# A graph layer on one core: a reordered setup, a shorter end and three more picks

## The chip, the cores and the metric

The kernel runs on one core of a Trainium2 chip. The metric is the device time of one execution in microseconds (us); a comparison is of medians over several runs.

## What is computed

There are 6250 nodes with 64 features, 200000 edges sorted by destination, 32 attributes and 9 further numbers per edge. For every edge the kernel takes the source node's row, weighs it, projects it, and sums over the edges of a destination; a gate, a residual and a layer normalisation follow.

```python
w   = silu(edge_attr @ W1 + b1) @ W2 + b2                  # (E, 9)
msg = einsum('ef,em,fmg->eg', x[src], edge_sh * w, W_tp)   # (E, 64)
agg = segment_sum(msg, dst, N) / sqrt(16.0)                # AVG_DEG = 100000 / 6250
gamma, beta = split(silu(c_noise[:, None] @ Wn1 + bn1) @ Wn2 + bn2, 2)
out = layernorm(x + agg * (1 + gamma) + beta)
```

## The kernel before

The edges lie in 1563 tiles of 128 (one edge to a partition), and the tiles in 98 blocks of 16 (`KB`). A block's source rows come into `hs[g]`, 128 x 16 x 64, in three ways:

- Most tiles are fetched by GpSimd with an indirect DMA of 128 rows each (`gather`, L99). Gathers run ahead of use by up to `AHEAD` = 6 blocks, in seven buffers; a gather of block g needs the buffer of block g-7, which `windows` (L533) has to have read.
- In every fourth block from block 7 on, one tile's rows are fetched one by one from the SP queue (`load_rows`, L115), 32 rows in each of four blocks.
- The last `picked(g)` tiles of a block, up to `Q` = 4, are "picked" out of a copy of x that lies in SBUF (`xs_w`, split into a high and a low part): a source index is cut into a key (partition, and one of 7 groups) and a place `jl` (one of 7). `hots` (L485, VectorE) compares the key of each edge with partition numbers and gives seven one-hot matrices `hot_k`; `pick` (L500, TensorE) multiplies them with `xs` in 14 matmuls of 448 columns into `px`; VectorE masks with `jl` (L509) and reduces (L511) into `hs`. `px` has two buffers.

The rest of a block: `hidden` (L429) and `hidden_act` (L438) are the first layer of the edge network, `second` (L447, L450) the second, `weights` (L457 to L467) turns and multiplies it into `a`, with the one-hot place of the destination in a window of 7 nodes (`near`, L408, from `rel`). `windows` (L533, L543) multiplies each tile's rows with `a`; `project` (L573, L579) applies W_tp to a pair of blocks, `halves` and `marks` make `r` and the one-hot `hot`, `place` (L595) puts the sums of a pair in their node columns, transposed, adding what the pair before carried over (`carry`, `yt`), and `bring` (L612) turns them back to nodes on partitions, where `finish` does gate, residual and normalisation and stores.

The order of instructions on each engine is the order of the program text (`manual_schedule`). Iteration i of the block loop issues the gathers of block i+6, the keys and `hots` of block i+2, pick 0 of block i+1 with the node work `nodes(i)` between its matmuls, `hidden(i+2)`, `second(i+1)`, `windows(i)`, `project` for odd i, and the other picks of block i+1.

The key table: `keys_of` works the keys out on VectorE in ten operations. Those of blocks 0 and 1 are spread over partitions by a matmul with `ones` (`keys_first`); those of all other blocks are transposed in three parts (`keys_rest`), written to DRAM (`kd`), and read back for two blocks at a time, spread over partitions (`load_keys`); `keys` copies them into PSUM. `setup` does all of this before the loop begins, together with the split of x (`split`, L247, L248), the first three picks (those of block 0), the tables for the window start of each block (`nid`, from `first_f`, `sel`, `lo`), and `rel` of all blocks.

At the end, after the picks of block 97, the pair (95, 96) is projected and placed, `bring` finishes two node tiles, and then block 97 goes the same way alone for the last node tile.

Of the kernel before, what the change touches and what calls it, by code (L numbers as in the profile page):

```python
# [7 lines left out]
F32 = mybir.dt.float32  # L8
# [8 lines left out]
P = 128  # L17
# [6 lines left out]
W = 7  # L24
# [27 lines left out]
def picked(g):  # L52

    return Q - (g % 5 == 0)
# [13 lines left out]
def gnn_resnorm_kernel(ctx: ExitStack, tc: tile.TileContext, x, src, dst, dst_row, ea, sh, cn,  # L68
# [18 lines left out]
    with ExitStack() as fast:  # L87
# [58 lines left out]

        def setup(temp):
# [12 lines left out]
            row_i = xb.rearrange("p j f -> p (j f)")[:, 0:NBLK * KB].bitcast(I32)  # L160
            load(0, split=True)
            nc.sync.dma_start(dst_i[:, 0:2 * KB], dst[:, 0:2 * KB])
            nc.sync.dma_start(row_i[:, 0:2 * KB], rows(dst[0, 0:2 * KB], P))
# [5 lines left out]
            for c in range(KB // 4):  # L169
                q = c * D  # L170
                nc.sync.dma_start(b2c[q:q + 2 * M, :], bass.AP(tensor=b2.tensor, offset=b2.offset,
                                                               ap=[[0, 2], [1, M], [1, 1]]))
            first_i = temp.tile([NBLK, KB], I32)
            nc.sync.dma_start(first_i, dst[0].rearrange("(g k) -> g k", k=KB))
            cn_j = temp.tile([NJ, P], F32)
            nc.sync.dma_start(cn_j, cn)

# [4 lines left out]
            sel_i = temp.tile([KB, P], I32)  # L182
# [5 lines left out]
            for g in range(AHEAD):  # L188
                gather(g)

# [6 lines left out]
            nc.vector.tensor_copy(li, n_i[:, 0:J])  # L197
            ones = temp.tile([P, P], F32)
            nc.vector.memset(ones, 1.0)


            zt_r = ztw

            def keys_of(g0, g1):

                c0, c1 = g0 * Q, g1 * Q
                s_f, kp, kh, rest, t0, t1 = [zt_r[:, k * C + c0:k * C + c1] for k in range(6)]
                ti = [t.bitcast(I32) for t in (t0, t1)]
                g2 = min(g1, NBLK - 1)
                nc.vector.tensor_copy(s_f[:, 0:(g2 - g0) * Q].rearrange("p (g k) -> p g k", k=Q),  # L210
                                      src_i.rearrange("p (g k) -> p g k", k=KB)[:, g0:g2, KB - Q:])
                if g1 == NBLK:
                    nc.vector.tensor_copy(s_f[:, (g2 - g0) * Q:], src_i[:, NT - Q:NT])
                nc.vector.tensor_scalar(ti[0], s_f, 2675.0, None, op0=ALU.mult)
                nc.vector.tensor_scalar(ti[0], ti[0], 17, None, op0=ALU.logical_shift_right)
                nc.vector.tensor_copy(kp, ti[0])
                nc.vector.scalar_tensor_tensor(rest, kp, -float(J * J), s_f, op0=ALU.mult, op1=ALU.add)
                nc.vector.tensor_scalar(ti[1], rest, 37.0, None, op0=ALU.mult)
                nc.vector.tensor_scalar(ti[1], ti[1], 8, None, op0=ALU.logical_shift_right)
                nc.vector.tensor_scalar(kh, ti[1], float(P), None, op0=ALU.mult)  # L220
                nc.vector.tensor_add(s_f, kp, kh)
                nc.vector.scalar_tensor_tensor(jl[:, c0:c1], kh, -float(J) / P, rest, op0=ALU.mult, op1=ALU.add)
                return s_f

            def keys_first(g, kf, tag):

                pk_t[g] = psum.tile([P, Q, P], F32, tag=tag, name=f"pk{g}")
                for t in range(picked(g)):
                    c = (g + 1) * Q - picked(g) + t
                    d0 = NBLK * KB + c * P  # L230
                    dg = xb.rearrange("p j f -> p (j f)")[:, d0:d0 + P]
                    nc.vector.tensor_scalar(dg, ident, kf[:, c:c + 1], None, op0=ALU.mult)
                    nc.tensor.matmul(pk_t[g][:, t, :], ones, dg, start=True, stop=True)  # L233

            def keys_rest(kf):
                for c0 in range(LB * Q, C, P):
                    n = min(P, C - c0)
                    p_kt = psum.tile([P, P], F32, tag="r", name=f"p_kt{c0}")
                    nc.tensor.transpose(p_kt[0:n], kf[:, c0 - LB * Q:c0 - LB * Q + n], ident)
                    kt = zt_r[:, 6 * C + c0 // 2:6 * C + c0 // 2 + P // 2].bitcast(F16)  # L240
                    nc.scalar.copy(kt[0:n], p_kt[0:n])
                    nc.sync.dma_start(kd[c0:c0 + n, :], kt[0:n])


            def split(h):
                xh = gam[:, h * J:(h + 1) * J, :].rearrange("p l f -> p f l")
                nc.scalar.copy(xs[0][:, h], xh)  # L247
                nc.vector.tensor_sub(xs[1][:, h], xh, xs[0][:, h].bitcast(F32))  # L248

            kf = keys_of(0, LB)  # L250
            keys_first(0, kf, "r")
            hots(0, 0, 1)
            for h in range(J):
                split(h)
                if h == J // 2:
                    hots(0, 1, 2)
            one = temp.tile([1, 1], F32)
            nc.vector.memset(one, 0.0)
            nc.scalar.activation(one, one, AF.Silu)
            pick(0, 0)  # L260
            hots(0, 2, Q)
            hidden(0)
            keys_first(1, kf, "s")
            hots(1, 0, 1)
            nc.vector.tensor_copy(wi, n_i[:, 0:W])
            nc.vector.tensor_sub(rel[:, 0:2 * KB], dst_i[:, 0:2 * KB], row_i[:, 0:2 * KB])
            near(0)
            pick(0, 1)
            hots(1, 1, Q)
            second(0)  # L270
            pick(0, 2, [[lambda: None, lambda: None], weights(0)])
            hidden(1)

            nc.sync.dma_start(dst_i[:, 2 * KB:], dst[:, 2 * KB:])
            nc.sync.dma_start(row_i[:, 2 * KB:], rows(dst[0, 2 * KB:], P))
            load(LB)
            keys_rest(keys_of(LB, NBLK))
            load_keys(LB)
            for q in range(2):
                n = (M + 1 - q) // 2  # L280
                nc.sync.dma_start(wtc2[q * F:(q + 1) * F, 0:n, :], wtp[:, q:M:2, :])
            nc.vector.memset(wtc2[F:P, 4], 0.0)
            zero = temp.tile([P, 1], F32)
            nc.vector.memset(zero, 0.0)
            nc.scalar.copy(zt[F:P, :, 4].rearrange("p a k w -> p a (k w)"),
                           zero[F:P, :, None].to_broadcast([F, 4, KW]))
            nc.sync.dma_start(wn1c, wn1.rearrange("o h -> h o"))
            nc.sync.dma_start(bn1c, bn1.unsqueeze(1))
            nc.sync.dma_start(wn2a[0:H, :], wn2)
            nc.sync.dma_start(wn2a[H:H + 1, :], bn2.unsqueeze(0))  # L290
            row_f = temp.tile([P, len(SPG)], F32)
            nc.vector.tensor_scalar(row_f, src_i[:, SPG[0] * KB:NBLK * KB:SPS * KB], 4.0 * F, None, op0=ALU.mult)
            p_row = psum.tile([len(SPG), P], F32, tag="s", name="p_row")
            nc.tensor.transpose(p_row, row_f, ident)
            nc.vector.tensor_copy(row_a, p_row)
            first_t = temp.tile([NBLK, KB], F32)
            nc.scalar.copy(first_t, first_i)
            p_f = psum.tile([KB, NBLK], F32, tag="s", name="p_f")
            nc.tensor.matmul(p_f, first_t, ident[0:NBLK, 0:NBLK], start=True, stop=True)
            nc.scalar.copy(first_f, p_f)  # L300
            p_cn = psum.tile([P, NJ], F32, tag="r", name="p_cn")
            nc.tensor.matmul(p_cn, cn_j, ident[0:NJ, 0:NJ], start=True, stop=True)
            cn_s = temp.tile([P, NJ], F32)
            nc.scalar.copy(cn_s, p_cn)
            nc.sync.dma_start(cn_d, cn_s)
            gate_load(0)

            nc.vector.tensor_copy(lo, lo_i)
            sel_a = temp.tile([KB, P], F32)
            nc.vector.tensor_scalar(sel_a, sel_i, -0.5, None, op0=ALU.is_gt)  # L310
            sel = temp.tile([KB, P], F32)
            nc.vector.scalar_tensor_tensor(sel, sel_i, W - 0.5, sel_a, op0=ALU.is_lt, op1=ALU.mult)
# [6 lines left out]
            p_nid = psum.tile([P, NBLK], F32, tag="s", name="p_nid")  # L319
            nc.tensor.matmul(p_nid, sel, first_f, start=True, stop=True)  # L320
            nc.vector.scalar_tensor_tensor(nid, p_nid, pw, lo, op0=ALU.add, op1=ALU.subtract)
            nc.vector.tensor_add(ident2, ident[:, 0:F], ident[:, F:P])
            for k in range(2):
                nc.vector.memset(ht[k][H:H + 1], 1.0)
            nc.vector.memset(eps, EPS)

            nc.vector.tensor_sub(rel[:, 2 * KB:], dst_i[:, 2 * KB:], row_i[:, 2 * KB:])
            nc.vector.memset(rel[:, NT:], 0.0)
            if E % P:
                nc.vector.memset(rel[E % P:, NT - 1:NT], 0.0)  # L330
# [307 lines left out]
        with tc.manual_schedule(), tc.tile_pool(name="temp", bufs=1) as temp:  # L638
            setup(temp)

            for i in range(NBLK):
# [4 lines left out]
                if i % LB == 0 and i + LB < NBLK:  # L646
                    if i > 0:
                        load(i + LB)
# [261 lines left out]
```

## Time and profile before

| | |
|---|---|
| runs, median (3) | 1493.0 us (1492.52 to 1494.01) |
| profiled execution: own time, span | 2388.12 us, 2386.3 us |
| mean granted TensorE clock in it | 0.841 |
| busy: PE, PEld, DVE, ACT, POOL | 1675.3, 1367.1, 1206.6, 521.1, 1109.7 us |
| pick matmuls (L500), gathers (L99), row fetches (L115) | 5208, 1168, 2944 |
| DMA queue of SP (q1) | 52122 packets, 53.89 MB |

How to read it: PE is TensorE's matmuls, PEld its weight loads, DVE is VectorE, ACT ScalarE, POOL GpSimd, SP the queue of plain DMAs. A group's line gives line, engine, operation, out<-in and count, then busy time and mean ns of one, then idle time of the engine before it and what ended most of it. The profiled execution is 1.6 times as long as a run, so its spans aren't those of a run; its single durations are what is used.

### The profile page before, as it was taken

Reading aid. Unit: us, or ns where it says so; the run is one execution under the profiler, and the core shown is the slowest. Engines: PE = TensorE matmul, PEld = TensorE weight load, DVE = VectorE, ACT = ScalarE, POOL = GpSimd, SP = SyncE. Lnnn points to the kernel's source line nnn. Section 1 sums busy time; section 2 is a strip of 40 time slices with the busy share of each in tenths; the row PEclk is TensorE's granted clock in tenths of the full one; section 3 lists DMA queues with packets and bytes.
Section 4 is the critical chain, followed back from the end, with each engine's and each line's share of the span. In section 5 each row is a group of like instructions: output and inputs, shape, how many; then the busy total and the mean of one; then the engine's idle time right before and its main releaser. Section 6 shows DMA issues by size and latency. Waiting matters only on the chain. (4 is left out here: it accounts for less than half of the span.)

```text
span 2386.3 us, 34188 instructions
## 1 busy us (share of the span) xinstructions
PE 1675.3 (70%) x10858; PEld 1367.1 (57%) x10858; DVE 1206.6 (51%) x2157; ACT 521.1 (22%) x1326; POOL 1109.7 (47%) x1177
## 2 busy tenths in 40 slices
PE   3076777676776767677767677677777676877797
PEld 2065656564655655556656556565656564656586
DVE  3154545454545454545555545454545454545476
ACT  1021212121212121211222222121212121212133
POOL 7644444444444545444545454545444544444410
PEclk7598888888888988887888898788887888888898
DMA  3121111111111111111111111111111111111110
GB/s 114 34 62 40 47 34 41 36 46 37 38 35 42 41 39 38 44 37 38 35 36 44 38 37 45 35 36 35 47 34 37 36 45 35 37 35 46 33 38 5
DMA packets 90264, 96.13 MB, mean 40 GB/s; under 512 B 36744, under 2 KB 51290, under 8 KB 90074
## 3 DMA queue, kind: packets, MB, share of 16 engines
q1 hardware_dynamic: 52122, 53.89, 7.9%
q0 software_dynamic: 37376, 38.35, 7.1%
q8 instruction: 89, 1.46, 0.2%
q10 hardware_dynamic: 576, 1.61, 0.2%
q14 instruction: 101, 0.83, 0.1%
HBM read 92.01 MB, written 1.73 MB: 39 GB/s over the span
## 5 line engine op out<-in xcount | busy, mean ns | idle before, releaser
L99 POOL DMA_INDIRECT hs<-in_x_dram,src_i x1168 | 1108.4, 949 | 1167.6 <-PE pz L533 825.8
L500 PE MATMUL px<-xs_w,hot_k 128*128 128x448 f32 x5208 | 1304.3, 406 | 432.3 <-DVE xm L509 377.0
L500 PEld LDWEIGHTS px<-xs_w,hot_k 128*128 128x128 f32 x5208 | 1067.0, 213 | 567.4 <-DVE xm L509 409.5
L509 DVE SCALAR_TENSOR_TENSOR xm<-li,jl,px 128x448 f32<-128x448 f32 x372 | 251.8, 677 | 936.4 <-remote 698.0
L485 DVE TENSOR_TENSOR hot_k<-pk,nk 128x896 fp32r<-128x896 f32 x372 | 387.7, 1081 | 2.8 <-PE pk L233 2.8
L511 DVE TENSOR_REDUCE hs<-xm 128x64 f32<-128x448 f32 x372 | 230.6, 620 | 12.9
L438 ACT ACTIVATE st<-p,b1c 128x1024 f32<-128x1024 f32 x98 | 109.2, 1115 | 542.4 <-PE p L429 365.3
L543 ACT COPY ztw<-pz 64x140 f32<-64x140 f32 (+1 forms) x780 | 209.2, 268 | 21.7 <-PE pz L533 10.3
L447 PE MATMUL p<-st,w2p 128*32 128x256 f32 x784 | 71.8, 430 | 152.4 <-DVE xb L370 102.9
L601 ACT COPY carry<-ps 128x128 f32<-128x128 f32 x48 | 12.8, 266 | 649.4 <-PE ps L595 587.0
L533 PEld LDWEIGHTS pz<-a,hs 128*64 128x64 f32 x3116 | 116.5, 155 | 58.7 <-issue 55.1
L447 PEld LDWEIGHTS p<-st,w2p 128*32 128x32 f32 x784 | 17.6, 113 | 228.7 <-issue 127.1
L533 PE MATMUL pz<-a,hs 128*64 128x63 f32 x3116 | 131.7, 244 | 11.7 <-issue 11.5
L467 DVE TENSOR_TENSOR a<-oh,p 128x1008 f32<-128x1008 f32 x98 | 117.9, 1203 | 3.3
L429 PE MATMUL p<-ea,w1bd 64*128 64x512 f32 x392 | 111.5, 642 | 0.7 <-issue 0.7
L728 ACT ACTIVATE var<-var,eps 128x2 f32<-128x2 f32 (+1 forms) x25 | 7.4, 295 | 374.6 <-DVE var L725 374.6
L579 PE MATMUL pt<-ztw,wtc 128*64 128x112 f32 x960 | 71.9, 308 | 18.6 <-ACT st L438 18.6
L579 PEld LDWEIGHTS pt<-ztw,wtc 128*64 128x64 f32 x960 | 61.7, 170 | 20.6 <-ACT st L438 20.3
L554 DVE TENSOR_TENSOR r<-pt,r 112x128 fp32r<-112x128 f32 x48 | 13.9, 289 | 97.2 <-issue 86.2
L479 ACT CAST pk<-kr 128x512 f32<-128x512 f16 (+1 forms) x96 | 54.6, 569 | 16.5 <-DVE hot_k L485 11.1
L450 ACT ACTIVATE p2s<-p,b2c 128x256 f32<-128x256 f32 x98 | 45.9, 468 | 48.6 <-issue 30.5
L457 DVE STREAM_TRANSPOSE p<-p2s 128x256 f32<-128x256 f32 x98 | 44.1, 450 | 14.9 <-issue 14.4
(138 smaller groups left out, 552.7 us busy)
## 6 DMA issues: line engine op xcount, KB each, us to landing
hs<-in_x_dram SPq DMA_DIRECT2D x2944, 0.2 KB
ea<-in_ea_dram SPq DMA_DIRECT2D x48, 512.0 KB
hs<-in_x_dram,src_i POOLq DMA_INDIRECT x1168
kr<-kd SPq DMA_DIRECT2D x48, 256.0 KB
sh<-in_sh_dram SPq DMA_DIRECT2D x49, 144.0 KB
cb<-cn_d SPq DMA_DIRECT2D x12, 128.0 KB
out_dram<-o SPq DMA_DIRECT2D x24, 64.0 KB
dst_i<-in_dst_dram SPq DMA_DIRECT2D x1, 768.0 KB
```

The source lines that it names most:

```text
L99: hs_dma[g] = [nc.gpsimd.indirect_dma_start(out=hs[g][:, t - g * KB, :], out_offset=None, in_=x, in_offset=bass.IndirectOffsetOnAxis(ap=sr ...
L429: nc.tensor.matmul(p1[:, i, :].rearrange("p (c t e) -> p c t e", c=4, t=4), w1bd[i * 64:(i + 1) * 64, :], e[i * 64:(i + 1) * 64, :].rearra ...
L438: nc.scalar.activation(st[g], p1_t.pop(g), AF.Silu, bias=b1c)
L447: nc.tensor.matmul(p2[g][c * D:(c + 1) * D, 0, :].rearrange("p (i e) -> p i e", i=2), w2p, s[:, :, c * P:(c + 1) * P], start=True, stop=True)
L467: nc.vector.tensor_mul(a[g], oh_t.pop(g)[:, :, None, :].to_broadcast([P, KB, M, W]), sw.unsqueeze(3).to_broadcast([P, KB, M, W]))
L485: nc.vector.tensor_tensor(hot_k[g, t], pk_t[g][:, t, None, :].to_broadcast([P, J, P]), nk.unsqueeze(2).to_broadcast([P, J, P]), op=ALU.is_ ...
L500: nc.tensor.matmul(px.rearrange("p f l -> p (f l)"), hot_k[g, t][:, h, :], xs[i][:, h].rearrange("p f l -> p (f l)"), start=(h == 0 and i ...
L509: nc.vector.scalar_tensor_tensor(xm, li[:, None, :].to_broadcast([P, F, J]), jl[:, c:c + 1], px, op0=ALU.is_equal, op1=ALU.mult)
L511: nc.vector.tensor_reduce(hs[g][:, tiles(g) - q + t, :], xm, AX.X, ALU.add)
L533: mm = nc.tensor.matmul(pz[v][v * F:(v + 1) * F, k // 2].rearrange("p m w -> p (m w)"), hsg[:, k0 + k, :], ag[:, k0 + k].rearrange("p m w ...
L543: nc.scalar.copy(z[h * F:(h + 1) * F, 0:5 - h, k0 + v:k0 + n:2, :].rearrange("p m k w -> p k m w"), pz[v][v * F:(v + 1) * F, 0:(n + 1 - v) ...
L579: nc.tensor.matmul(pt[h * F:(h + 1) * F, 0, 0:KW], wtc2[:, c, :], z[h][:, c], start=(c == 0), stop=(c == 4))
```

## The change

It has five parts. `picked` leaves out one pick in every sixth block where it was every fifth. `keys_of` becomes a list of operations that work on a given buffer of six columns, `keys_rest` is replaced by `keys_turn`, one transpose of 128 keys; setup does only the keys of blocks 2 to 33, and those of 34 to 65 and 66 to 97 are worked out in iterations 2 and 4 of the loop, between picks, and transposed at the end of iterations 3 and 5. `rel` is worked out for blocks 0 and 1, then to block 9 in setup (`relative`), and for the others in iteration 6; its row numbers lie in `gam` instead of `xb`. `setup` takes in what was iteration 0 of the loop, so that the picks of blocks 0 and 1 stand among the setup's other work; `split` reads x in order and writes with a step, where it read with a step and wrote in order. At the end, block 97 is not placed and brought back: the sums of the pair (95, 96) and of block 97 are made by matmuls with `hot` as the stationary side, which gives nodes on partitions directly, and the last two node tiles are finished in one go.

```diff
-    return Q - (g % 5 == 0)
+    return Q - (g % 6 == 0)
...
+        def keys_turn(g0, kf, tag, kt):
+            c0 = g0 * Q
+            p_kt = psum.tile([P, P], F32, tag=tag, name=f"p_kt{g0}", bufs=1 + (tag == "pz"))
+            nc.tensor.transpose(p_kt, kf, ident)
+            nc.scalar.copy(kt, p_kt)
+            stores.append(lambda: nc.sync.dma_start(kd[c0:c0 + P, :], kt))
...
+        row_r = gam.rearrange("p j f -> p (j f)")[:, NBLK * KB:2 * NBLK * KB].bitcast(I32)
+        KC = P // Q
+        KN = 10 * KB
...
-            for g in range(AHEAD):
+            for g in range(AHEAD + 1):
                 gather(g)
...
             def split(h):
-                xh = gam[:, h * J:(h + 1) * J, :].rearrange("p l f -> p f l")
-                nc.scalar.copy(xs[0][:, h], xh)
-                nc.vector.tensor_sub(xs[1][:, h], xh, xs[0][:, h].bitcast(F32))
+                xh = gam[:, h * J:(h + 1) * J, :]
+                hi, lo_ = [xs[i][:, h].rearrange("p f l -> p l f") for i in range(2)]
+                nc.scalar.copy(hi, xh)
+                nc.vector.tensor_sub(lo_, xh, hi.bitcast(F32))
...
+            kb = [ztw[:, k * LB * Q:(k + 1) * LB * Q] for k in range(6)]
+            for f in keys_of(0, LB, kb):
+                f()
+            for f in keys_first(0, kb[0], "pz"):
+                f()
+            spread = keys_first(1, kb[0], "r")
...
+            hots(0, 0, 1)
+            for h in range(J):
+                split(h)
+            nc.scalar.activation(one, one, AF.Silu)
+            nc.sync.dma_start(dst_i[:, 2 * KB:], dst[:, 2 * KB:])
+            nc.sync.dma_start(row_r[:, 2 * KB:], rows(dst[0, 2 * KB:], P))
+            hots(0, 1, 2)
+            pick(0, 0, [spread[0:4], [lambda: hidden(0)]])
+            hots(0, 2, Q)
...
+            pick(0, 1)
+            second(0)
+            hots(1, 0, 1)
...
+            for f in keys_of(LB, LB + KC, kb):
+                f()
+            pick(0, 2)
+            hidden(1, act=False)
+            kt = temp.tile([P, P], F16)
+            keys_turn(LB, kb[0], "pz", kt)
+            hidden_act(1)
+            while stores:
+                stores.pop(0)()
+            load_keys(LB)
...
+            hots(1, 1, 2)
+            pick(1, 0)
+            nc.vector.tensor_copy(row_a, p_row)
+            nc.vector.tensor_sub(rel[:, 0:2 * KB], dst_i[:, 0:2 * KB], row_i)
+            near(0)
...
+            for f in weights(0):
+                f()
...
+            hots(1, 2, 3)
+            pick(1, 1)
...
+            windows(0)
+            second(1)
+            hots(1, 3, Q)
+            keys(2)
...
+            pick(1, 2)
+            hidden(2)
+            hots(2, 0, 1)
+            for f in weights(1):
+                f()
+            hots(2, 1, 2)
+            pick(1, 3)
+            relative(2 * KB, KN)
+            near(2)
+            hots(2, 2, Q)
...
+            more_of = {2: keys_of(LB + KC, LB + 2 * KC, kb), 4: keys_of(LB + 2 * KC, NBLK, kb),
+                       6: [lambda k=k: relative(KN + k, min(KN + k + 352, NBLK * KB))
+                           for k in range(0, NBLK * KB - KN, 352)]}
-            for i in range(NBLK):
+            for i in range(1, NBLK):
...
-                for t in range(2, Q):
-                    pick(i + 1, t)
+                beside = more_of.pop(i, [])
+                n = -(-len(beside) // (Q - 1))
+                for t in range(2, Q + 1):
+                    for f in beside[(t - 2) * n:(t - 1) * n]:
+                        f()
+                    if t < Q:
+                        pick(i + 1, t)
+                if i in (3, 5):
+                    keys_turn(LB + KC * (i - 1) // 2, kb[0], "s", kt)
...
-            pick(g, 2)
+            for f in bring(q - 2, q - 1, psum.tile([P, 1, F], F32, tag="r", name="py_l"), ends):
+                f()
+            windows(g - 1)
             sums(g)
-            windows(g - 1)
-            pick(g, 3)
-            marks(g // 2)
-            turn = project(g // 2)
+            pick(g, 2, [ends])
+            pick(g, 3, [project(q)])
...
+            py = psum.tile([P, FB, F], F32, tag="s", name="py_n")
+            nc.tensor.matmul(py[:, 0], carry.pop(q - 1), ident2, start=True, stop=False)
+            for b in range(2):
+                for k, h in enumerate(pair(q)):
+                    for s in range(2):
+                        nc.tensor.matmul(py[:, b], hot[h][:, b * P:(b + 1) * P], r[q][:, k, s],
+                                         start=(b == 1 and k == 0 and s == 0), stop=(b == 0 and k == 1 and s == 1))
+            windows(g, [0])
+            marks(NJ)
             windows(g, [ZT])
...
+            z = zs.pop(g).rearrange("p c k w -> p c (k w)")
+            pr = psum.tile([P, F], F32, tag="r", name="pr_n")
+            for c in range(5):
+                nc.tensor.matmul(pr[0:KW], z[:, c], wtc2[:, c, :], start=(c == 0), stop=(c == 4))
+            last = work.tile([KW, F], F32, tag="rt", name="last")
+            nc.vector.tensor_copy(last, pr[0:KW])
+            nc.tensor.matmul(py[:, 1], hot[g][:, 0:P].bitcast(F32), last, start=False, stop=True)
+            finish(q - 1, NJ, py)
```

Left out of the diff are the new places in the SP queue: the loads for blocks 2 and 3, W_tp and the gate's weights go out right after the first small loads, before the gathers are issued; the rest of `dst` and its row numbers follow the last split; the key part, `cn_d`, x for the residual (`xb`), `w2bd` and `b2r` follow within the picks of blocks 0 and 1. The tables `sel`, `pw` and `wi` move ahead of the first comparison, the rows of ones in `ht` are written by ScalarE instead of VectorE, and in `windows` of block 97 two of the copies of the second half go to VectorE.

## The prediction

> **What bounds the kernel now.** I read four views: the page, the waits, the timeline of the start and of the end, and a table of windows. First, the totals do not fit the runs: the profiled execution took 2388.1 us (span 2386.3, 1.8 around it), the runs 1493.0. The page and the waits say what the 895 us are.
>
> ```profile
> PE 1675.3 (70%) x10858; PEld 1367.1 (57%) x10858; DVE 1206.6 (51%) x2157; ACT 521.1 (22%) x1326; POOL 1109.7 (47%) x1177
> ...
> L99 POOL DMA_INDIRECT hs<-in_x_dram,src_i x1168 | 1108.4, 949 | 1167.6 <-PE pz L533 825.8
> L500 PE MATMUL px<-xs_w,hot_k 128*128 128x448 f32 x5208 | 1304.3, 406 | 432.3 <-DVE xm L509 377.0
> ```
> ```profile
> DVE xm L509 <- remote: 698.0, 119, 36.4
> ```
>
> PE is busy longer than a whole run lasts, and DVE waits 698 us for a releaser the trace cannot name. The timeline shows one such wait: PE has ended the pick's matmuls at 41.5, DVE reads them at 88.2.
>
> ```profile
> 36.33 5.16 PE L500 MATMUL px<-xs_w,hot_k 128*128 128x448 f32 x14
> ...
> 88.18 0.68 DVE L509 SCALAR_TENSOR_TENSOR xm<-li,jl,px 128x448 f32<-128x448 f32 x1 [36.45 <-remote]
> ```
>
> After such a wait PE is also slow: 14 matmuls in 5.16 us, against 3.05 at 20 us. So these waits belong to the profiled execution (1493 us has no room for them), and I take durations only where they are absent: the last 120 us, where PE has no gap.
>
> ```profile
> 2300.40:2314.50 14.10, 14.10 (x103) 11.90 (x102) 11.29 (x17) 3.87 (x12) 0.00 (x0) 1.00 0.25 67
> 2314.50:2330.00 15.50, 15.50 (x128) 13.13 (x127) 11.28 (x21) 4.82 (x15) 0.00 (x0) 1.00 0.00 1
> ```
> ```profile
> 2301.41 11.47 PE L500 MATMUL px<-xs_w,hot_k 128*128 128x448 f32 x56
> 2312.82 1.13 PE L429 MATMUL p<-ea,w1bd 64*128 64x512 f32 x4
> ```
>
> Columns of the first fence: stretch, its length, busy time of PE, PEld, DVE, ACT, POOL, clock. PE fills both blocks at clock 1.00. From the second: four picks (56 matmuls) run from 2301.41 to 2312.52 (0.3 us of gap before L429), so **a pick is 2.78 us of PE**. Between the pz of four blocks (2282.91 to 2341.69) lie 15 picks and 58.8 us: 14.70 a block, 14.84 at the kernel's 3.80 picks; one wait for an activation table load and st (1.6) in it, so 14.44 without. Blocks below 51 add the gate product (24.3 us in 49), 0.25 on the mean: 14.7 to 15.1.
>
> Two paths follow. **PE**: block loop from i=1 at 57.3 (worked out below), 95 blocks, then 33.3 from pick(97,0) at 2353 to the end, and 1.8: 1488 to 1526. **POOL**: gathers follow each other at 1.2534 us (mean of the 1075 unhindered intervals); 3.97 + 1168 x 1.2534 = 1468, 2 to land, then 14.7 from the last pz[0] to the end and 1.8: 1486.5. The median 1493 lies in the first and 6.5 above the second. So PE sets the end, POOL is close behind: its 14.9 a block gives it the rows of block i at about 19 + 14.9 i, PE asks at 48 + 14.75 i.
>
> **What the Trainium skill says.** "TensorE: Matmul & The Clock Gate", section "Wait — 56ns, not 53.3ns?": warm matmuls start N/2.4 GHz plus 2.5 ns apart, 189 ns for 448 columns, and cold ones at half the clock, 373. The trace: 198 in the last stage, 369 after the long wait. "DMA: Bandwidth & Descriptors", section "Anatomy of one DMA": some 2 us of a transfer are fixed, mostly the receipt of the write. No transfer's landing in this setup is measured in what I read; I use 2 us for the key table's way out to DRAM. "SBUF — State Buffer", section "Door 1: The DMA port swizzle": an access that crosses to a new 16-byte line pays. `split` reads at 256-byte steps now (0.93 us of DVE for 448 values, xm takes 0.68); afterwards it writes and re-reads at 28-byte steps, which cross too. No run shows that price.
>
> **Part 1: three more picks.** picked(g) sums to 372 now and 375 then (20 blocks short of one before, 17 after). PE: 3 x 2.78 = **+8.3**. DVE: 3 x (1.08 + 0.68 + 0.62) = 7.1, beside PE (DVE is busy 11.3 of 14.1 us in a block without finish). POOL: 3 gathers less, -3.8, off PE's path.
>
> **Part 2: the setup.** I lay out both orders with trace durations, without the long waits.
> Before: pick(0,0) ends on PE at 16.3. DVE then has xm and reduce of three picks (3.9), five hot_k (5.2), diagonals 0.9, near and small 0.7, weights(0) 2.2: 12.9, with 1.6 of waits for picks, 30.8. Key table of 384 columns, ten operations: 4.9, 35.7. Three transposes and ACT copies one behind the other on one PSUM tag (about 1 us each), kd written (2 us), read back: kr at about 44. Meanwhile DVE: row_a, nid behind p_f and p_nid, ht memsets 1.03, rel 1.75: 45.0. Then i=0: near 0.4, hot_k of block 2 4.2, xm(1,0) 1.3, weights(1) 2.2; PE ends pick(1,3) at **57.3**. Loop i=1 with project(0): 16.4, i=2: 14.9, so i=3 starts at 88.6.
> After: key diagonals of block 1, sel and pw lie in DVE idle time ahead of hot_k(0,0) (ends 9.0 for 8.8); seven splits in a row to 15.1; hot_k(0,1) 16.2. Then DVE is nearly solid: three xm 3.9, hot_k 2.1, keys of 128 columns 2.6, by 25.9; one hot_k, xm(1,0), row_a, rel of 32 columns, near, weights(0) by 33.1; two hot_k, xm(1,1), nid, by 37.1; xm(1,2), weights(1), two hot_k, xm(1,3) by 47.4; rel of 128 columns, near(2), hot_k(2,2..3), ident2 by 50.4. PE, ahead, ends pick(1,3) at **44.5**. The key table leaves at 25.4 and is needed at 37.1: its 4 to 5 us are covered by 11.7. PSUM tag "pz" holds pk0, p_kt, p_row, p_f, p_cn, p_nid in turn; windows(0) waits some 1.5 us for nid behind it, counted. The ht memsets go to ACT as two copies (0.6 each, by the 0.56 of zt's 448) ahead of st(2), while PE is in pick(1,2): hidden.
> Given back: DVE is 6 us behind PE, and pick(2,3) waits for xm(2,1). i=1 takes 18.2, i=2 15.1 (2.6 of DVE keys beside picks, DVE still 1.8 behind), so i=3 starts at 77.8: **10.8 earlier**. The keys at i=4 (2.6) and rel at i=6 (four of about 0.5) lie in DVE's 1.4 a block of room and the px buffers; if that cover is gone, up to 3. The two late transposes are 0.5 each on PE: **-9.8** in sum. Range -6 (splits slower by 0.3 each on DVE, kr at once before, the late keys uncovered) to -13 (splits at xm's 0.68, kr later before).
> SP: load(2), wtc and wn go out ahead of rest of dst and row; the write of a key third waits at the top of i=4 and i=6 for its copy, and behind it load(i+2) and 32 row fetches (10.8 us a block, L115) wait. Loads are for two blocks on, fetches for three to six: hidden, 1 us at most. The dst rest waits for the last split (gam is reused), 35 us ahead of use. POOL: the seventh group's gathers come from setup, same order, nothing.
>
> **Part 3: the end.** After pick(97,3) (PE 2366.5) the profile runs
>
> ```profile
> 2369.82 0.52 PE ps_l L595 x2
> ...
> 2371.01 0.66 PE py_l L612 x4
> ...
> 2373.49 2.14 PE pr L573 x10
> ...
> 2376.24 0.60 PE ps_n L595
> ...
> 2377.20 0.70 PE py_n L612 x2
> ```
> to 2386.3: 19.8 us, each step waiting for the one ahead (the chain of waits). After: xm and reduce 1.4, beside them carry, eight matmuls and windows(97,[0]), about 2.0; windows [8] 0.3; copies 1.1; pr 2.14; copy 0.25; last matmul 0.7; finish of two tiles 3.0 (as 2371.7 to 2374.7); store 5.9 as now (2380.4 to 2386.3): 15.5. Saved 4.3. But project(48) 1.2, its turn 0.3 and bring 0.35 move ahead of pick(97,3): +1.85. **-2.4**, bounds -1 to -3.5 (the eight products have no row; ps L595 takes 0.28 for 256 columns, I take 0.1 each).
>
> **Sum.** +8.3 - 9.8 - 2.4 = -3.9. Median 1493.0, so **1489**. Taken on the profiled 2388.1 the same edits would be 2384, but its remote waits (698 us) can move by more.
>
> **Rivals.**
> 1. PE as above: 1489, its own range 1484.5 (-13, -3.5) to 1494.5 (-6, -1, picks 8.6). For it: PE without a gap. Chance 0.5.
> 2. POOL already sets the end (gathers a little slower in a run than in the profile): then only its 3 x 1.25 and 0.5 of the tail count, 1488.7. Against: 6.5 us of room. Chance 0.17.
> 3. Start held up more than I laid out, as in the profile, where PE idles 42.6 to 93.9: the new order takes that away, up to where POOL binds: 3.97 + 1165 x 1.2534 + 2 + 14.2 + 1.8 = 1482. Against: the old kernel would then end beyond 1493. Chance 0.13.
> 4. Slower: DVE's debt is not paid. Each pick of i=1 to 6 waits in px (two buffers) for an xm behind hot_k, weights and keys; 5.2 us of keys and 1.9 of rel go on PE's path with setup's 6. s falls to 4, the end to -1.5: 8.3 - 5.5 = +2.8, 1496. It decides from s + e below 8.3 less 3.0. For it: DVE's 13.4 of 14.8 a block with finish and gates. Against: 1.4 a block repays. Chance 0.2.
> That the picks do not move is excluded: the sum over blocks is arithmetic.
>
> **Numbers.** About 0.2% (3 us) is what a measurement of this kernel tells from no change. Case 1 gives faster 0.32, same 0.17, slower 0.01; case 2 0.14 and 0.03; case 3 faster; case 4 same 0.04, slower 0.16: together 0.59, 0.24, 0.17. Range 1482 to 1497.
>
> **What would show it.** 5250 px matmuls and 1165 gathers; first pz L533 earlier against the number of picks ahead of it; PE without gaps in the last 100 us at 14.7 a block; from the last px to the end 15 to 16 us, with no ps or yt step. Wrong if DVE xm holds px in the first blocks beyond i=3, if splits take over 1.2 us, or if POOL no longer waits for pz near the end.

## The result, and the profile after

The changed kernel takes 1489.2 us (median of 20 runs, 1487.8 to 1494.1), the kernel before beside it 1493.3 (20 runs): ratio 0.9975, 95% interval 0.9969 to 0.9981, so 4 us less, against 3.9 predicted. In the first two sets of runs below every kernel, the one before included, took about 2400 us, in all others about 1490, on the same chip too, so each ratio is taken to the kernel before in the same set. The profiled execution took 1488.34 us with a span of 1486.5, that is 1.8 around it, at a mean granted clock of 0.994: unlike that of before, it is an execution like the runs, and its totals can be read.

On the page of the kernel after, first busy times, then the two groups that answer to those of before (busy, mean ns, idle before and releaser):

```profile
PE 1443.6 (97%) x10905; PEld 1211.5 (82%) x10905; DVE 1210.6 (81%) x2188; ACT 515.7 (35%) x1324; POOL 1108.5 (75%) x1174
...
L99 POOL DMA_INDIRECT hs<-in_x_dram,src_i x1165 | 1107.2, 950 | 357.1 <-issue 321.1
L536 PE MATMUL px<-xs_w,hot_k 128*128 128x448 f32 x5250 | 1125.2, 368 | 1.5 <-DVE hot_k L521 1.4
```

PE is busy for 97% of the span and the picks wait for next to nothing. But L99 tells of a second full queue: its 357 us of idle time are "issue", 0.3 us between one gather and the next, and no longer a wait for `pz`. GpSimd issues without a pause from 4.0 us to its last gather at 1465.2. Two queues are full at once here, and most of what the experiments showed follows from that.

In the waits of the kernel after (us in total, times, longest), the `remote` wait of 698 us is gone, and these are the two PE waits that come up again below:

```profile
PE pr L610 <- issue: 5.8, 1, 5.8
...
PE p L465 <- DMA ea<-in_ea_dram: 2.3, 2, 1.4
```

The timeline of PE in the kernel after, at the end (start, us, what, and the wait ahead of it):

```profile
1469.24 1.86 PE L536 MATMUL px<-xs_w,hot_k 128*128 128x448 f32 x8
...
1471.08 1.06 PE L743 MATMUL py_n<-r,c 112*128 112x64 f32 x8
...
1474.37 2.13 PE L751 MATMUL pr_n<-wtc,ztw 128*112 128x64 f32 x10 [1.40 <-ACT ztw L580]
1476.82 0.69 PE L754 MATMUL py_n<-last,c 112*128 112x64 f32 x2 [0.32 <-DVE last L753]
```

The `ps` and `yt` steps of before are gone; `py_n` is made by matmuls with `hot` (here `c`) directly. From the last pick (1471.1) to the end of the span (1486.5) pass 15.4 us, predicted 15.5.

### The profile page after: what moved, and what is told of

It reads as the page before. It is cut to its first block, busy times and chain, and to the rows that moved or that the text cites. A ratio compares the mean times of both kernels' runs of the same rounds, so it can differ in the third digit from the quotient of the medians.

```text
span 1486.5 us, 34308 instructions
## 1 busy us (share of the span) xinstructions
PE 1443.6 (97%) x10905; PEld 1211.5 (82%) x10905; DVE 1210.6 (81%) x2188; ACT 515.7 (35%) x1324; POOL 1108.5 (75%) x1174
## 3 DMA queue, kind: packets, MB, share of 16 engines
q1 hardware_dynamic: 52122, 53.89, 12.5%
## 4 chain that ended last, share of the span: by engine, by line
PE 79%; POOL 5%; DVE 5%; issue 4%; DMA 3%; ACT 3%; SPq 2%; ACTq 0%; DVEq 0%; POOLq 0%
PE px L536 60%; PE pz L569 6%; POOL hs L99 5%; PE p L465 5%; PE pt L616 3%; PE p L483 3%; DMA hs<-in_x_dram,src_i 2%; SPq L115 1%; ACT st L474 1%; DVE xm L545 1%; ACT L474 1%; PE ps L632 1%; DVE hs L547 1%; PE ps L661 1%; DVE hot_k L521 0%
## 5 line engine op out<-in xcount | busy, mean ns | idle before, releaser
L99 POOL DMA_INDIRECT hs<-in_x_dram,src_i x1165 | 1107.2, 950 | 357.1 <-issue 321.1
L536 PE MATMUL px<-xs_w,hot_k 128*128 128x448 f32 x5250 | 1125.2, 368 | 1.5 <-DVE hot_k L521 1.4
L536 PEld LDWEIGHTS px<-xs_w,hot_k 128*128 128x128 f32 x5250 | 961.2, 189 | 79.9 <-DVE xm L545 2.3
L569 PEld LDWEIGHTS pz<-a,hs 128*64 128x64 f32 x3116 | 99.6, 138 | 44.2 <-issue 39.3
L569 PE MATMUL pz<-a,hs 128*64 128x63 f32 x3116 | 112.8, 225 | 4.4 <-DMA hs<-in_x_dram,src_i 1.6
L483 PE MATMUL p<-st,w2p 128*32 128x256 f32 x784 | 62.6, 391 | 7.6 <-DVE xb L406 7.6
L616 PE MATMUL pt<-ztw,wtc 128*64 128x112 f32 x960 | 55.3, 261 | 3.1 <-ACT st L474 2.5
L465 PEld LDWEIGHTS p<-ea,w1bd 64*128 64x128 f32 x392 | 29.6, 185 | 31.5 <-issue 24.4
L497 DVE TENSOR_TENSOR p<-p,sh 128x72 f32<-128x72 f32 x196 | 47.3, 241 | 6.7
L616 PEld LDWEIGHTS pt<-ztw,wtc 128*64 128x64 f32 x960 | 46.8, 137 | 5.0 <-ACT st L474 3.9
```

The lines of the kernel that those rows point to most:

```text
L99: hs_dma[g] = [nc.gpsimd.indirect_dma_start(out=hs[g][:, t - g * KB, :], out_offset=None, in_=x, in_offset=bass.IndirectOffsetOnAxis(ap=sr ...
L465: nc.tensor.matmul(p1[:, i, :].rearrange("p (c t e) -> p c t e", c=4, t=4), w1bd[i * 64:(i + 1) * 64, :], e[i * 64:(i + 1) * 64, :].rearra ...
L483: nc.tensor.matmul(p2[g][c * D:(c + 1) * D, 0, :].rearrange("p (i e) -> p i e", i=2), w2p, s[:, :, c * P:(c + 1) * P], start=True, stop=True)
L536: nc.tensor.matmul(px.rearrange("p f l -> p (f l)"), hot_k[g, t][:, h, :], xs[i][:, h].rearrange("p f l -> p (f l)"), start=(h == 0 and i ...
L569: mm = nc.tensor.matmul(pz[v][v * F:(v + 1) * F, k // 2].rearrange("p m w -> p (m w)"), hsg[:, k0 + k, :], ag[:, k0 + k].rearrange("p m w ...
L616: nc.tensor.matmul(pt[h * F:(h + 1) * F, 0, 0:KW], wtc2[:, c, :], z[h][:, c], start=(c == 0), stop=(c == 4))
```

## The experiments

The sum of the prediction is tested by the last six experiments alone, at about 1490 us.

### The kernel before, profiled again

Edit: none.

> The kernel before, unchanged, to see one more profiled execution of it. My theory (the 895 us of the first profile are waits of that one execution): a span of about 1491 us, TensorE without long gaps, loop iteration 1 (first matmul of pick(2,0)) at 57 us and iteration 3 at 88.6; the last gather issued at about 1468 us and pz[0] of block 97 some 6 us after its rows have landed. Rival (the waits belong to the kernel): again above 2000 us, with VectorE waiting 36 us in the setup.

Measured: 2417.4 us, clock 0.831, the kernel before beside it 2423.0 in the median. Its waits (total, times, longest):

```profile
DVE xm L509 <- remote: 654.5, 112, 35.8
```

The wait came again, and the runs without a profile were as long. So it doesn't belong to the profiled execution alone, as the prediction had said, but to the whole set of runs. What holds PE's completions back there stays open: no run tells it apart.

### Parts of the change, where every kernel takes about 2400 us

The new numbers of picks in the kernel before, the old ones in the kernel after, and in the kernel after `pr` of a single block in another PSUM tag:

```diff
-    return Q - (g % 5 == 0)          # before, 375 picks (the kernel after with 372: the other way round)
+    return Q - (g % 6 == 0)
...
-                pr = psum.tile([P, 1, F], F32, tag="r", name=f"pr{q}")      # after, pr in p1
+                pr = psum.tile([P, 2, 4 * P], F32, tag="p1", name=f"pr{q}")[:, 0, 0:F].unsqueeze(1)
```

> The kernel before with the new pick count alone (375 for 372). TensorE sets the end (my theory): three picks more on its path, +8.3 us, about 1501.6. GpSimd sets the end (rival 2 of the prediction): three gathers less, -3.8 us, about 1489.5.

> The changed kernel with the old pick count (372). TensorE sets the end with GpSimd about 4 us behind (my theory after the changed kernel's profile: last gather at 1465.2, pz[0] of block 97 at 1472.1): TensorE would be 8.3 us earlier, GpSimd 3.8 later, so GpSimd takes over and the time stays within 1 us of 1489. TensorE alone: 1481. GpSimd sets the end already: +3.8, 1493.

> The changed kernel with the single-block product of project(0) in PSUM tag p1 in place of r. In the changed kernel's profile it starts at 53.95, 5.8 us after the pz of block 1, when hot_k of block 3 has been read out of the key tile that holds tag r. If that is the wait: it starts at about 49.6, TensorE is 4.3 us earlier from there, and since GpSimd leaves about 4 us at the end the time falls by 3 to 4 us, to about 1485.5. If GpSimd sets the end: no change, 1489. If the wait is for something else (weights, table): the product still starts at 54.

> The kernel before with the new pick count alone (375 for 372), again, on another occasion than e2. TensorE sets the end (my theory): three picks more on its path, +8.3 us on before. GpSimd sets the end (rival 2 of the prediction): three gathers less, -3.8 us. Its trace also shows the old setup and the old end: by my layout pick(2,0) starts on TensorE at 57 us, and 19.8 us lie between the last px and the end.

> The changed kernel with the product of project(0) in PSUM tag p1 in place of r, again, on another occasion than e4. If hot_k of block 3, reading the key tile in tag r, is what holds it for 5.8 us: it starts at about 49.6 in place of 53.95, TensorE is 4.3 us earlier from there, and as GpSimd leaves about 4 us at the end, the ratio to before falls from 0.9975 to about 0.995 (1485.5 us). If GpSimd sets the end already: 0.9975 as the changed kernel. If the wait is for something else, the product still starts at 54.

| | this, us | before, us | ratio, 95% interval |
|---|---|---|---|
| before, 375 picks | 2402.3 | 2423.0 | 0.9924 [0.9895, 0.9953] |
| after, 372 picks | 2424.4 | 2423.0 | 1.0032 [1.0009, 1.0054] |
| after, `pr` in p1 | 2409.8 | 2423.0 | 0.9938 [0.9914, 0.9961] |
| before, 375 picks, again | 2414.7 | 2420.5 | 0.9970 [0.9944, 0.9996] |
| after, `pr` in p1, again | 2412.3 | 2420.5 | 0.9972 [0.9942, 1.0002] |

Three more picks make the kernel before faster here, twice, where PE's sum says 8.3 us slower. Both forecasts of +8.3 missed; they were worked out for about 1490 us. Where DVE waits some 650 us in all for PE's completions, the end isn't set by PE's sum of durations, and these runs say nothing on that sum. The same edits follow at 1490 us.

### Picks alone, in both kernels

> The kernel before with the new pick count alone (375 for 372). TensorE sets the end (my theory): three picks more on its path, +8.3 us, ratio 1.0055. GpSimd sets the end (rival 2 of the prediction): three gathers less, -3.8 us, ratio 0.9975. Its trace also shows the old setup and the old end without long waits: by my layout pick(2,0) starts on TensorE at 57 us, pick(4,0) at 88.6, and 19.8 us lie between the last px and the end.

> The changed kernel with the old pick count (372), on a third occasion. In an execution near 1490 us: TensorE would be 8.3 us earlier and GpSimd 3.8 later, so GpSimd takes over and the ratio to before stays within 0.001 of 0.9975; if TensorE alone sets the end, 0.992; if GpSimd does already, 1.000. In an execution near 2400 us, as on the two occasions before: no more than 0.5% of difference, as e3.

The kernel before with 375 picks: 1501.7 us against 1493.0, ratio 1.0060 [1.0042, 1.0077], **+8.7** where 3 x 2.78 = 8.3 was worked out. PE sets the end of the kernel before, and a pick costs what its row says.

The kernel after with 372 picks: 1491.6 against 1493.7, ratio 0.9986 [0.9979, 0.9993]. PE has 8.3 us less to do than in the kernel after, and it gets **1.6 slower** (0.9986 against 0.9975; the two intervals just overlap). Within 0.001 of 0.9975 was expected, and both the 0.992 of PE alone and the 1.000 of GpSimd that sets the end already are excluded. In its profile PE waits 9.2 us in all ahead of `pz` after 1000 us, in the kernel after nothing. Here GpSimd, with 3 gathers more, has taken over. So the three picks aren't just a cost that the setup pays for: without them GpSimd caps what setup and end bring.

### How far behind PE is GpSimd?

Twelve more gathers, one in every second block from 30 to 52, into a tile that nothing reads:

```diff
+            if g in range(30, 54, 2):
+                nc.gpsimd.indirect_dma_start(
+                    out=more_rows[:, g // 2 % 4, :], out_offset=None, in_=x,
+                    in_offset=bass.IndirectOffsetOnAxis(ap=src_i[:, g * KB + 1:g * KB + 2], axis=0))
```

> The kernel before with 12 more gathers (blocks 30 to 52, every second; the rows go to a tile that nothing reads): 15.0 us more on GpSimd's queue, nothing on another engine. TensorE sets the end of the kernel before with GpSimd 6.5 us behind (my theory): +8.5 us, ratio 1.0057. GpSimd sets it (rival 2): +15, ratio 1.010. GpSimd has far more room than I worked out: 1.000.

> The changed kernel with the same 12 more gathers, 15.0 us on GpSimd's queue. TensorE sets the end with GpSimd 4 us behind: +11 on 1489.2, ratio to before 1.0049. GpSimd sets it: +15, 1.0075. TensorE alone with much room: 0.9975.

In the kernel before: 1507.6 against 1493.0, ratio 1.0094 [1.0077, 1.0112]. Of 12 x 1.25 = 15.0 us of gathers **14.6** come out. In the kernel after: 1502.4, ratio 1.0063 [1.0045, 1.0080], **13.2** more than its 1489.2. Both were expected to lose less. The first is the number forecast for rival 2 (GpSimd sets the end already), though three more picks have just shown PE to set it; the second interval takes in both of its forecasts. GpSimd has little room in either kernel, and a part of the loss is of another kind (below).

Where it binds can be read. I took for each block the start of its last gather on GpSimd and the first `pz` on PE. In the kernel before with 12 more gathers the waits ahead of `pz` from 1000 us on that the trace puts down to gathered rows lie at blocks 66, 70, 76, 80 and 90, and none after. The distance is least at or just behind the blocks divisible by 5 (in the kernel after: by 6): these have three picks, so a gather more, and PE comes a pick early and GpSimd a gather late. Block 97, where the prediction had closed GpSimd's path, has 7 gathers. The last gather of block 90 and its first `pz`, in the timelines of GpSimd and PE of that kernel, then the same of the kernel after with 372 picks, and of the kernel after; last, the same `pz` of the kernel before with 375 picks:

```profile
1384.01 0.94 POOL L99 DMA_INDIRECT hs<-in_x_dram,src_i  x1 [0.30 <-issue]
...
1387.36 1.98 PE L538 MATMUL pz<-a,hs 128*64 128x63 f32 x32 [2.71 <-DMA hs<-in_x_dram,src_i]
```
```profile
1373.21 0.94 POOL L99 DMA_INDIRECT hs<-in_x_dram,src_i  x1 [0.30 <-issue]
...
1376.77 1.15 PE L569 MATMUL pz<-a,hs 128*64 128x63 f32 x32 [2.90 <-issue]
```
```profile
1367.69 0.94 POOL L99 DMA_INDIRECT hs<-in_x_dram,src_i  x1 [0.30 <-issue]
...
1372.59 1.15 PE L569 MATMUL pz<-a,hs 128*64 128x63 f32 x32
```
```profile
1382.56 1.15 PE L533 MATMUL pz<-a,hs 128*64 128x63 f32 x32
```

From the gather's end (1384.95, 1374.15, 1368.63) to `pz` pass 2.4 us in the first, with a wait of 2.71; 2.6 in the second, with a wait of 2.90 that has no named releaser but lies at the same place; 4.0 in the third, with none. The shortest such distance in these traces is 1.7 us, and the longest at which `pz` was still waiting for rows is 2.9 (block 66 of the kernel after with 12 more gathers), so rows can be used 1.7 to 2.9 us after their gather's end. In this profile the kernel after has 1.1 to 2.3 us of room at block 90, and its loss of 13.2 of 15.0 (10.4 to 15.7 by its interval) fits.

For the kernel before it can be worked out. With the 15.0 taken off, its last gather of block 90 starts at 1369.0, and its rows are there at 1371.6 to 1372.8. From `pz` at 1382.56 to the end of the span at 1499.2 pass 116.6 us in the kernel before with 375 picks, which waits for no rows there (the picks from there on are as many); so PE, ending at 1493.0 less 1.8, was at block 90 at 1374.6. Room: **2 to 3 us, and not 6.5**.

A wait here can cost more than its length. The granted clock in four stretches around block 90 of the kernel before with 12 more gathers (stretch, length, busy time of PE, PEld, DVE, ACT, POOL, clock, DMA share, GB/s):

```profile
1382.00:1387.30 5.30, 2.65 (x18) 1.08 (x16) 5.27 (x7) 1.48 (x2) 4.08 (x5) 0.96 0.34 75
1387.30:1391.00 3.70, 3.64 (x37) 3.40 (x38) 1.82 (x4) 2.38 (x9) 2.78 (x4) 0.50 0.16 33
1391.00:1395.00 4.00, 4.00 (x15) 3.62 (x14) 0.57 (x1) 1.52 (x2) 3.03 (x4) 0.66 0.14 26
1395.00:1400.00 5.00, 5.00 (x26) 4.53 (x25) 2.03 (x4) 0.00 (x0) 3.78 (x4) 1.00 0.15 27
```

After 2.7 us of waiting PE runs at half its clock; `pz` and the 44 pick matmuls behind it take 13.2 us to their end at 1400.6, against 10.2 at full clock (1.08 and 9.08 in the kernel before with 375 picks). So 3 us follow the wait, and they aren't made good. The waits ahead of `pz` after 1000 us add up to 12.5, with these 3 that is 15.5; the profiled execution took 1509.3, which is 16.3 more than 1493.0, the median 14.6. Not every wait does this: in the traces with more gathers the clock stayed at 1.00 behind waits of 2.11, 2.16 and 2.26 us, and fell to 0.62 behind one of 2.15.

### The DVE debt

> The changed kernel with the product of project(0) in PSUM tag p1 in place of r. If hot_k of block 3, reading the key tile in tag r, is what holds it for 5.8 us: it starts at about 49.6 in place of 53.95, TensorE is 4.3 us earlier from there, and as GpSimd leaves about 4 us at the end, the ratio to before falls from 0.9975 to about 0.995 (1485.5 us). If GpSimd sets the end already: 0.9975, as the changed kernel. If the wait is for something else, the product still starts at 54.

Measured 1487.5 us against 1493.0, ratio 0.9960 [0.9945, 0.9974], faster than the kernel before. It is 1.7 us under the kernel after, which the overlapping intervals don't tell apart, where 3.7 was expected. PE in the kernel after, around the first `project`, with DVE's comparison that it waits for; then the same place with `pr` in p1:

```profile
47.00 1.15 PE L569 MATMUL pz<-a,hs 128*64 128x63 f32 x32
...
51.77 2.08 DVE L521 TENSOR_TENSOR hot_k<-pk,nk 128x896 fp32r<-128x896 f32 x2
...
53.95 2.10 PE L610 MATMUL pr<-wtc,ztw 128*112 128x64 f32 x10 [5.80 <-issue]
55.80 9.97 PE L536 MATMUL px<-xs_w,hot_k 128*128 128x448 f32 x44
```
```profile
49.47 1.15 PE L569 MATMUL pz<-a,hs 128*64 128x63 f32 x32
52.12 1.49 PE L610 MATMUL pr<-wtc,ztw 128*112 128x64 f32 x10 [1.50 <-ACT st L474]
```

In the kernel after `pr` takes PSUM tag "r", which holds the key tile of block 3 until DVE's last comparison has read it, at 53.85. PE stands still for 5.8 us. With another tag the wait is 1.5, so 4.3 shorter. In that profile the gain is less because PE came to this place 2.5 us later: 0.9 of it from further up, the rest after its clock had fallen to 0.54 from 35.6 to 38.0 us, where the kernel after had 1.00. Whether the timed runs share that isn't known. GpSimd, 1.1 to 2.3 us behind in the kernel after, leaves little more to gain.

### The old end in the kernel after

The lines from the last `pick(g, 2)` on, and the copies of `windows` for block 97, as in the kernel before; setup and picks as after.

> The kernel after with the old ending of the last blocks (the folded copies in the windows too), its setup and its 375 picks kept. Theory (the PE sets the end of the kernel after, GpSimd 1.6 us behind): the new end was worth 4.3 us after the last px, less 1.85 us of its work that it put ahead, so 2.4 us are lost: 1491.6 where the kernel after gave 1489.2, ratio to the kernel before 0.9989. Rival (GpSimd sets the end of the kernel after too): the tail after the last gathered block is what counts, and it is 14.7 against 14.4 us: 0.5 us at most, ratio 0.9977. Rival (the work put ahead was hidden): the full 4.3 us, 1493.5, ratio 1.0001.

Measured 1493.7 us against 1495.5 on that chip, ratio 0.9989 [0.9983, 0.9996], as the first theory had it: 2.1 us more than the kernel after (0.9989 - 0.9975 = 0.0014, by 1493). PE at the end of this kernel:

```profile
1474.03 0.51 PE L631 MATMUL ps_l<-c,r 112*128 112x256 f32 x2 [1.28 <-DVE r L590]
1475.22 1.04 PE L647 MATMUL py_l<-ident,yt 128*128 128x64 f32 x4 [0.68 <-DVE yt L640]
...
1481.24 0.58 PE L631 MATMUL ps_n<-c,r 112*128 112x256 f32 x1 [0.62 <-DVE r L590]
1482.21 0.69 PE L647 MATMUL py_n<-ident,yt 128*128 128x64 f32 x2 [0.39 <-DVE yt L640]
```

These are the steps that the new end does without: two of `ps` and two of `py` behind the last picks, each behind a copy on another engine. The gain is the difference of the tails less what was put ahead of the last pick, not the raw 4.3, which the interval excludes. So does it exclude the rival's 0.5 at most. But that forecast let GpSimd bind at the last block. Had it bound at block 90, the whole of the old end would still lie on PE's path behind it, so this run alone doesn't tell who sets the end. The traces do: after 1000 us no `pz` waits for gathered rows in the profile of the kernel after, nor in this one.

## Why the prediction was right

The size came out, and so did the mechanism: PE set the end before (8.7 us for three picks) and sets it after (no wait for rows), and the sum of the three parts holds. The time alone would not have shown it, since rival 2 forecast 1488.7. With the same 375 picks, the kernel after is 12.5 us under the kernel before (1501.7 - 1489.2), where -9.8 and -2.4 were worked out. The profiles split it at the first `pz` of block 90, up to which both kernels have the same picks: PE is there 10.0 us earlier (1382.56 and 1372.59), and 2.8 shorter from there to the end (116.6 and 113.9). Step by step:

**Picks.** +8.3 predicted, +8.7 measured.

**Setup.** The timeline of PE in the kernel before with 375 picks (up to 92 us its picks are those of the kernel before), and in the kernel after:

```profile
44.49 5.32 PE L500 MATMUL px<-xs_w,hot_k 128*128 128x448 f32 x14
...
52.45 11.47 PE L500 MATMUL px<-xs_w,hot_k 128*128 128x448 f32 x56
...
67.84 1.17 PE L573 MATMUL pr<-wtc,ztw 128*112 128x64 f32 x10 [1.20 <-issue]
68.81 9.06 PE L500 MATMUL px<-xs_w,hot_k 128*128 128x448 f32 x44
...
83.27 9.08 PE L500 MATMUL px<-xs_w,hot_k 128*128 128x448 f32 x44
```
```profile
39.41 6.03 PE L536 MATMUL px<-xs_w,hot_k 128*128 128x448 f32 x28
...
71.18 9.08 PE L536 MATMUL px<-xs_w,hot_k 128*128 128x448 f32 x44
```

A run of 44 holds three picks and the first two matmuls of the next, so the next pick starts 0.5 us ahead of its end; in the run of 56 the fourth pick, and in that of 28 the second, is (2,0).

| pick that starts | before: laid out, measured | after: laid out, measured | lead: predicted, measured |
|---|---|---|---|
| (2,0) | 57.3, 60.6 | 44.5, 42.3 | 12.8, 18.3 |
| (3,0) | 73.7, 77.3 | 62.7, 65.2 | 11.0, 12.1 |
| (4,0) | 88.6, 91.7 | 77.8, 79.7 | 10.8, 12.0 |

The old setup is 3 us later than I laid out, and 2.3 of that is the clock: pick (1,0), the first line above, runs at a granted clock of 0.50, from 47 us on 0.61, after long waits and takes 5.32 us, where 3.05 is usual. The new setup is 2 us earlier and then 2 us later, and the lead that is left at i=3 is 1.2 larger than predicted. The late transposes take 0.27 each, and at 100.3 PE waits 1.4 us for `ea`. 12.0 - 0.5 - 1.4 is 10.1, and 10.0 is what is left at block 90, for 9.8 predicted. That the sum is nearer than its terms is luck: the errors cancel.

**The DVE debt** was foreseen in its kind and wrong in its place. It was to be paid by pick (2,3) waiting in `px`; it is paid at `project(0)`, which the PSUM tag of the key tile holds for 5.8 us, and after that PE had lost its clock as well, as three stretches of the kernel after show (columns as above):

```profile
53.90:57.00 3.10, 3.05 (x13) 3.00 (x14) 0.68 (x3) 0.92 (x3) 2.35 (x3) 0.50 0.12 25
57.00:60.00 3.00, 3.00 (x14) 2.75 (x14) 2.10 (x5) 0.49 (x2) 2.37 (x3) 0.87 0.67 230
60.00:64.00 4.00, 4.00 (x21) 3.76 (x21) 2.42 (x4) 0.00 (x0) 2.83 (x3) 1.00 0.19 45
```

`pr` and the 44 matmuls behind it end 11.8 us after `pr` starts (53.95 to 65.77), 10.0 in the kernel before with 375 picks (67.84 to 77.87). So i=1 takes 22.9 us for 18.2, 1.8 of which is clock. The Trainium skill has it in "TensorE: Matmul & The Clock Gate", section "What's actually happening": half the clock after an idle window of about 3.4 us, full again after a busy one. The trace agrees for this wait of 5.8. But a wait of 2.7 was enough at block 90, and with `pr` in p1 the clock fell at 35.6 after a stretch of 3.6 us in which PE worked for 2.3; in the kernel after PE worked for as long in that stretch, and its clock stayed at 1.00. So the length of a wait doesn't decide by itself, and what does isn't shown. The prediction priced waits at their length alone, in the old setup too.

**Splits.** 0.93 each was taken for both, with 0.3 either way. In the undisturbed traces the old form has a median of 949 ns (kernel before with 375 picks), the new one 983 ns: to write with a step costs 0.03 us more than to read with one, 0.2 in all.

**The key table.** Its way out to DRAM was priced at 2 us, from the Trainium skill's "DMA: Bandwidth & Descriptors", section "Anatomy of one DMA", which is on transfers that GpSimd issues, while this one goes out from SP. The write is issued at 25.29 and the read-back at 26.79, 1.5 later, and `windows(0)` at 34.2 waits 1.3 us for ScalarE's copies and for nothing of the key table: hidden, as said. The wait for `nid` that was counted (1.5) didn't come; this one did in its place.

**The end.** The tail from the last pick is 19.7 us in the kernel before with 375 picks (1479.5 to 1499.2; 19.8 predicted) and 15.4 after (15.5), the loss without it 2.1 (2.4).

**The room of GpSimd** is the term that was mis-sized: 6.5 us, where the runs show 2 to 3 before and 1.1 to 2.3 after. The step that failed is its path, closed at the last block by 14.7 us from the last `pz[0]`. Block 97 has 7 gathers where others have 11 to 13, so GpSimd is early there; it is block 90, with 13, where PE is 2 to 3 us behind the rows, and from there PE has 116.6 us to go by itself.

A second term was put at nothing: the gathers in the setup ("same order, nothing"). GpSimd and VectorE in the kernel after, then in the kernel before with 375 picks:

```profile
8.91 6.46 DVE L278 TENSOR_TENSOR xs_w<-gam,xs_w 128x448 fp32r<-128x448 f32 x7
...
11.01 5.18 POOL L99 DMA_INDIRECT hs<-in_x_dram,src_i  x1 [0.30 <-issue]
```
```profile
8.77 3.53 DVE L248 TENSOR_TENSOR xs_w<-gam,xs_w 128x448 fp32r<-128x448 f32 x4
...
10.78 1.43 POOL L99 DMA_INDIRECT hs<-in_x_dram,src_i  x1 [0.30 <-issue]
```

One gather takes 5.18 us there instead of 1.43. The first gather starts at 4.0 to 4.1 us everywhere, the 51st at 70.2 to 72.7 in the five profiles with the new setup at 1490 us, at 69.1 and 69.6 in the two with the old one; and with the same 1165 gathers the last starts at 1465.2 in the kernel after and at 1462.8 in the kernel before with 375 picks. So the new setup itself takes 2.5 us of GpSimd's room in this profile. Each time the slow gathers end 0.2 us before VectorE has come through the seven splits and the comparison behind them (16.2 and 16.4 us in the kernel after). The splits write with a step now and stand in a row, where the old order had four, a comparison and three; whether either holds the gathers is not shown, for no run takes it back alone.

For these two reasons rival 3's bound of 1482 was no bound: GpSimd's path gives about 1487.5 in the kernel after (1489.2 less its room). Rival 2, in which GpSimd sets the end already, was nearer than its 0.17 said; it is excluded by the +8.7 for the kernel before, and for the kernel after by its trace. The prediction named as a sign of being wrong that POOL no longer waits for `pz` near the end. That sign came true, and it was a bad sign: by the prediction's own figures PE asks for a block's rows at most 29 us after GpSimd has them, where the buffers allow six blocks, and GpSimd doesn't wait for `pz` in the kernel before with 375 picks either. The 825.8 us of such waits belong to the 2400 us.

**The profiled 2388 us.** That the 895 us "belong to the profiled execution" is wrong, as the first experiment showed. The single durations taken from where the waits were absent held all the same.

Why the change brings 4 us and not more can then be said. Setup and end free 12.5 us of PE; three picks take 8.3 to 8.7 of it, and with GpSimd 3 gathers shorter, both queues come down. The kernel after with 372 picks has PE's path at 1480.9 (1489.2 - 8.3) and takes 1491.6, as GpSimd then holds it: 1487.5, and 3 x 1.25 for the gathers that come back, that is about 1491.2.

## What to carry to other kernels

Where two queues run side by side, price each edit on both, and close the second path at every place where they meet, above all at the block in which one has most to do and the other least: here that was block 90 of 98, and the last block had room to spare. A saving on the first queue is worth only the room of the second, so, as the three picks do here, move work from the second to the first with the time that was freed. A wait for a PSUM tag is a wait for all that its last holder is read by, as `pr` waited for the key tile's comparison: look through who holds each tag when work is moved forward. And look at the second queue in the stretch that was rearranged, even where its own order is the same.

## What the runs showed of the hardware

- A TensorE wait can cost more than its length: after 2.7 us of waiting the granted clock was 0.50 for 3.7 us, then 0.66 for 4, and 3 us were lost behind it; after a wait of 5.8 us 1.8 were lost. Waits of 2.1 to 2.3 us had it both ways, clock 1.00 in three cases and 0.62 in one.
- The rows of an indirect DMA of 128 rows could be used 1.7 to 2.9 us after the instruction's end on GpSimd, and such instructions follow each other at 1.25 us (0.94 and 0.30).
- While VectorE ran the seven splits that write with a step and a comparison (8.9 to 16.4 us), one such instruction took 5.18 us (6.80 and 6.95 in two other runs), and 1.43 while it ran those that read with a step. The cause isn't shown.
